# Two more products of h's part of n placed between the copy of the first gate product's bank and its second use

## The chip, the cores and the metric

The kernel runs on one core of one Trainium2 chip. The metric is the device time of one execution in microseconds (us). The time before is the median of three runs.

## What is computed

The reference has two layers over 128 graphs of 128 nodes with 256 features, all in float32. The change lies in the last step of layer 0, a gated unit. Cut to that part:

```python
h = relu(layernorm(x))
x_conv = ...                      # a convolution over the nodes of h
x_nmp  = ...                      # messages weighted by exp(-distance)
gi = concat([x_conv, x_nmp]) @ w_ih.T + b_ih
gh = h @ w_hh.T + b_hh
r = sigmoid(gi_r + gh_r)
z = sigmoid(gi_z + gh_z)
n = tanh(gi_n + r * gh_n)
x = x + (1 - z) * n + z * h
```

So r and z need one sum of three products each (of h, of the convolution and of the messages), while n needs h's product (gh_n) apart from the other two, because r multiplies it. "h's part of n" is that product, gh_n. Layer 1 is a graph convolution over 25 nodes of each graph.

## The kernel before, in words

The graphs are taken in 32 groups of four. `stage_c(q)` computes the gated unit of group q. The left operands are features on partitions, so h, the messages and the convolution of a group are tiles `hT`, `xm` and `xc` of 128 partitions by 2 by 512.

Each product of a 2 by 2 block weight matrix with a 2 by 2 block activation is done as seven products of sums of blocks in place of eight products of blocks. The sums of weights are made once (`fold_gates`: `wrz` for r and z, `wn` for n from messages and convolution, `wh` for n from h). The sums of activations are made per group on VectorE (`sums`: tiles `th`, `tm`, `tc`). In `stage_c`, `part(ps, w, i, xs, first, last)` issues the matmuls of product i into a PSUM bank `ps`, and `product` takes a bank and does a whole product in it. `factor` chooses the block or the sum for slot i. One matmul of 128 rows by 256 columns in float32 is two instructions in the profile. A part of `wrz` over one source is two matmuls (four instructions), and a product of `wh`, which has one source and half the width, is one matmul (two instructions).

PSUM has three banks in the pool `pgat` (the gates' banks `p1`, `p6`, `p5`, and later products in the same three) and five in the pool `ptmp` (tag "tmp"), which all other work shares.

The order around the change, by the lines of the kernel before:

- L741: product 0 of the r and z gates is ended in bank `p1`, by the convolution's part of it.
- L742: ScalarE copies `p1` to `u2`, because product 0 is wanted alone as well.
- L743 to L745: VectorE makes the four sums `tc` of the convolution.
- L757 to L759: product 0 of h's part of n is made in the bank `h1` (from `ptmp`), and ScalarE copies it to `va`.
- L761: product 1 of the gates is added into the same bank `p1` (its second use), over h, messages and convolution: six matmuls, twelve instructions.
- L762: ScalarE takes the sigmoid of `p1`, which gives the first half of r.
- L764 to L766: product 5 is ended in `p6`, VectorE adds it to `u2`; product 1 of h's part of n is added into `h1`, and `gate` multiplies it with r.
- L769 and L770: product 4 is ended in `p5`; product 5 of h's part of n is made and VectorE adds it to `va`.
- L777 to L780: product 6 of the gates is made, VectorE forms `u3` and `z2`; product 6 of h's part of n is made and VectorE writes `vb = va + product`.
- L785 to L796: products 3, 2 and 4 follow, product 2 in bank `p5` for the second time.

The copies `u2` share their SBUF place (tags `u2`, `u3`) with the tiles `d` of the step's end (L832 to L836), which GpSimd reads.

The order of the whole program is written out when it is built. Each piece of work is a generator in a `Lane`, and `Order.run` picks the lane that has had the least TensorE time for its weight, among those that are due. A `yield a, b` says that the piece has put a microseconds of work on TensorE and is due again b microseconds later. So the numbers in the yields decide where the other lanes' instructions are placed between the pieces of `stage_c`: the rest of the message work (`early`), the normalization before layer 1 (`rows`) and layer 1 itself (`prepare`, `block`). In the transposes that end group q-1 (`po`, L853) the same lane comes back to an earlier group.

Of the kernel before, what the change touches and what calls it, by code (L numbers as in the profile page):

```python
# [11 lines left out]
ALU = mybir.AluOpType  # L12
# [195 lines left out]
def kernel(ctx: ExitStack, tc: tile.TileContext, x, adj, consts, vecs, w_se, conv1_w,  # L208
                    conv2_w, w_msg, b_msg, w_ih, w_hh, W1, W2, b2, fusion_w, out):
    nc = tc.nc  # L210
# [7 lines left out]
    ptmp = ctx.enter_context(tc.tile_pool(name="ptmp", bufs=5, space=PSUM))  # L218
# [336 lines left out]
    def some_sums(q, n):  # L555

        if q in IN:
            if q not in SUMS:
                hT, xm = IN[q]
                (th, a), (tm, b) = sums("th", q, hT), sums("tm", q, xm)  # L560
                SUMS[q] = th, tm, a + b
            while SUMS[q][2] and n != 0:
                SUMS[q][2].pop(0)()
                n = n and n - 1
# [92 lines left out]
    def stage_c(q):  # L657
# [38 lines left out]
        wrz, wn, wh = LATE["wrz"], LATE["wn"], LATE["wh"]  # L696
# [6 lines left out]
        def part(ps, w, i, xs, first, last, again=False):  # L703


            n = [(m, o) for o in xs for m in range(w.shape[3] // P)]
            for j, (m, (k, x, t)) in enumerate(n):
                nc.tensor.matmul(ps[:, m], w[:, i, k, m * P:(m + 1) * P], factor(i, x, t),  # L708
                                 start=first and j == 0, stop=last and j == len(n) - 1,
                                 skip_group_check=again)  # L710

        def product(w, i, xs, pool=pgat):
            ps = bank(w, i, pool)
            part(ps, w, i, xs, True, True)
            return ps

        def bank(w, i, pool=pgat):
            return pool.tile([P, w.shape[3] // P, D], FP, tag="gat" if pool is pgat else "tmp",
                             name=f"p{w.shape[3]}{q}_{i}")

        def sigmoid(dst, src, b):
            for m in range(2):
                nc.scalar.activation(dst[:, m], src[:, m], AF.Sigmoid, bias=brz[:, b + m:b + m + 1])  # L723
# [23 lines left out]
        xs, xh = [(0, hT, th), (2, xm, tm), (1, xc, tcs)], [(0, hT, th)]  # L747

        ve = fr.tile([P, 3, 1, D], FP, tag="ve", name=f"ve{q}")
        va, vb, vt = ve[:, 0], ve[:, 1], ve[:, 2]  # L750
# [6 lines left out]
        h1 = bank(wh, 0, ptmp)  # L757
        part(h1, wh, 0, xh, True, True)
        nc.scalar.activation(va, h1, AF.Copy)  # L759
        yield 0.43, 0.0  # L760
        part(p1, wrz, 1, xs, False, True, True)  # L761
        sigmoid(r1, p1, 0)  # L762
        yield 2.6, 0.0
# [3 lines left out]
        gate(r11, h1, 0)  # L767
        yield 1.3, 0.0
        part(p5, wrz, 4, xs[2:], False, True)  # L769
        nc.vector.tensor_tensor(va, va, product(wh, 5, xh, ptmp), ALU.add)  # L770
        some_sums(q + 1, 2)
        yield 1.3, 0.0
        while q and q - 1 not in C_DONE:
            yield 0.0, 0.5
        z = fr.tile([P, 2, 512], FP, tag="z", name=f"z{q}")
# [1 line left out]
        nc.vector.tensor_tensor(u3, u2, product(wrz, 6, xs), ALU.add)  # L777
        nc.vector.tensor_tensor(z2, u3, p5, ALU.add)  # L778
        sigmoid(z2, z2, 2)
        nc.vector.tensor_tensor(vb, va, product(wh, 6, xh, ptmp), ALU.add)  # L780
        some_sums(q + 1, 2)
        yield 3.03, 0.0
        xt = fr.tile([P, 4, D], FP, tag="xt", name=f"xt{q}")
        load_x(xt, q)
        nc.vector.tensor_tensor(z1, u3, product(wrz, 3, xs), ALU.add)  # L785
# [322 lines left out]
    for bat, (during_a, during_b) in enumerate(((0.66, 0.5), (0.2, 0.65))):  # L1108
# [12 lines left out]
        tc.tile_pool(name="co", bufs=1, side="right", reuse_waits="tile"))  # L1121
    loads = Lane([stage_n(q) for q in range(NQ)])
    groups = Lane([stage_c(q) for q in range(NQ)], ahead=2)
    second = [setup_1()] + [part(blk) for blk in range(NBLK) for part in (prepare, block)]
    beside.weight = 0.5
# [43 lines left out]
```

## Time and profile before

| what | value |
|---|---|
| three runs | 2124.36, 2126.18 and 2129.8 us, median 2126.18 us |
| profiled execution, its own time | 2123.29 us |
| its span in the profile | 2121.2 us |
| mean granted TensorE clock | 0.989 |
| TensorE: matmuls busy, weight loads busy | 2056.6 us (97%), 1656.3 us (78%) |
| VectorE, ScalarE, GpSimd busy | 1177.2 us (55%), 687.6 us (32%), 723.2 us (34%) |
| first and last copy `u2` (L742) | at 730.9 us and at 2001.6 us, 32 copies |

The page gives one profiled execution. The groups' gated units take the stretch from about 724 us to the end, with layer 1 interleaved. In the profile's rows, PE is a matmul and PEld is the loading of its weights; an idle time is followed by an arrow to what ended it. Instructions are named by line and by output<-input tile; `p<-hTc,wrz` is a matmul with h as the moving operand, out of `wrz`, into a gate's bank.

### The profile page before, as it was taken

How to read it: one execution, taken by the hardware profiler on the slowest of the kernel's cores; microseconds unless marked ns; L12 is line 12 of the kernel's file. 1: busy time of each engine (PE TensorE's matmuls, PEld its weight loads, DVE VectorE, ACT ScalarE, POOL GpSimd, SP SyncE). 2: the span in 40 equal slices, each digit the busy share in tenths (PEclk: the TensorE clock that was granted, in tenths of full speed). 3: DMA queues.
4: the chain of work that ended last, by engine and by line, in shares of the span. 5: the costliest groups of instructions: out<-in, count | busy, mean ns of one | idle time of the engine just before them, and what ended most of it. 6: DMA issues, size and time to landing. Idle time of an engine off the chain costs nothing.

```text
span 2121.2 us, 30965 instructions
## 1 busy us (share of the span) xinstructions
PE 2056.6 (97%) x11316; PEld 1656.3 (78%) x11316; DVE 1177.2 (55%) x2775; ACT 687.6 (32%) x1543; POOL 723.2 (34%) x900
## 2 busy tenths in 40 slices
PE   6998999999999999999999999999999999999998
PEld 5566888789888787787778777878787787778775
DVE  5665444786544455645654654566455555654542
ACT  3554222344222233332232332232233323223233
POOL 2442666231565123422332233233213323233230
PEclk9999999999999999999999999999999999999999
DMA  9997778744787534233223232323222332323121
GB/s 182 264 269 231 242 267 261 213 145 150 254 267 253 184 110 153 61 100 77 73 71 83 84 83 71 107 73 78 80 82 75 83 97 75 78 80 102 36 68 50
DMA packets 187050, 281.66 MB, mean 133 GB/s; under 512 B 20685, under 2 KB 140242, under 8 KB 186898
## 3 DMA queue, kind: packets, MB, share of 16 engines
q1 hardware_dynamic: 156066, 184.81, 31.2%
q0 software_dynamic: 30000, 94.13, 13.7%
q8 instruction: 90, 1.47, 0.3%
q10 hardware_dynamic: 832, 0.74, 0.2%
q14 instruction: 62, 0.51, 0.1%
HBM read 187.34 MB, written 92.27 MB: 132 GB/s over the span
## 4 chain that ended last, share of the span: by engine, by line
PE 88%; DVE 3%; DMA 3%; POOL 2%; ACT 2%; issue 1%; SPq 0%; POOLq 0%; DVEq 0%; ACTq 0%
PE p L708 39%; PE pa L501 7%; PE pm L600 5%; PE ph L1029 5%; PE pz L1038 5%; PE pc L397 4%; PE pb L501 3%; PE pf L408 3%; PE px L626 3%; PE pi L673 2%; PE pg L1072 1%; DMA wfd<-ws 1%; PE po L853 1%; PE ph L386 1%; PE pw L450 1%
## 5 line engine op out<-in xcount | busy, mean ns | idle before, releaser
L833 POOL TENSOR_TENSOR d<-hTc,r 128x512 f32<-128x512 f32 x64 | 81.4, 1272 | 371.1 <-ACT r L830 371.1
L501 PE MATMUL pa<-wf,X 128*128 128x256 f32 x640 | 152.4, 381 | 0.0
L862 POOL DMA_DIRECT2D out<-xt x128 | 71.8, 566 | 204.2 <-DVE xt L859 201.5
L723 ACT ACTIVATE z<-z,brz 128x256 f32<-128x256 f32 x128 | 58.1, 501 | 253.3 <-DVE z L778 205.6
L524 DVE SCALAR_TENSOR_TENSOR y<-pa,kk 128x512 f32<-128x512 f32 x78 | 53.8, 690 | 147.4 <-ACT kk L523 147.4
L708 PE MATMUL p<-th,wrz 128*128 128x256 f32 x512 | 131.8, 380 | 0.0
L708 PE MATMUL p<-tc,wrz 128*128 128x256 f32 x512 | 131.6, 379 | 0.0
L708 PE MATMUL p<-tm,wrz 128*128 128x256 f32 x512 | 131.4, 379 | 0.0
L501 PEld LDWEIGHTS pa<-wf,X 128*128 128x128 f32 x640 | 118.1, 190 | 16.4 <-issue 2.2
L397 PE MATMUL pc<-c1w,hTa 128*128 128x256 f32 x512 | 124.4, 389 | 3.5 <-ACT ef L588 2.3
L600 PE MATMUL pm<-wmsg,hT 128*128 128x256 f32 x512 | 124.0, 388 | 0.0
L690 DVE SCALAR_TENSOR_TENSOR xc<-pc,s_bn,hTc 128x256 f32<-128x256 f32 x128 | 53.1, 477 | 117.3 <-PE pc L687 117.3
L708 PE MATMUL p<-hTc,wrz 128*128 128x256 f32 x384 | 106.1, 399 | 10.1 <-ACT u L742 10.1
L397 PEld LDWEIGHTS pc<-c1w,hTa 128*128 128x128 f32 x512 | 95.3, 194 | 22.2 <-DVE h L400 4.0
L1029 PE MATMUL ph<-yz,w 128*128 128x96 f32 (+3 forms) x640 | 111.5, 329 | 0.9 <-DVE yz L1014 0.9
L708 PEld LDWEIGHTS p<-hTc,wrz 128*128 128x128 f32 x384 | 68.3, 191 | 55.6 <-ACT u L742 22.5
L600 PEld LDWEIGHTS pm<-wmsg,hT 128*128 128x128 f32 x512 | 97.4, 193 | 16.7 <-issue 1.6
L1031 ACT ACTIVATE hh<-ph,vec 128x96 f32<-128x96 f32 (+3 forms) x160 | 64.3, 403 | 139.8 <-PE ph L1029 130.9
L1038 PE MATMUL pz<-hh,w 128*128 128x96 f32 (+3 forms) x640 | 107.7, 322 | 0.0
L708 PEld LDWEIGHTS p<-tm,wrz 128*128 128x128 f32 x512 | 97.3, 190 | 13.2
L1029 PEld LDWEIGHTS ph<-yz,w 128*128 128x128 f32 x640 | 90.1, 197 | 21.8 <-issue 15.5
L708 PEld LDWEIGHTS p<-th,wrz 128*128 128x128 f32 x512 | 94.5, 190 | 12.6 <-issue 0.6
(203 smaller groups left out, 4590.4 us busy)
## 6 DMA issues: line engine op xcount, KB each, us to landing
wf<-wfd SPq DMA_DIRECT2D x160, 256.0 KB, 3.9
wfd<-ws POOLq DMA_DIRECT2D x64, 320.0 KB, 7.3
yd<-y POOLq DMA_DIRECT2D x80, 256.0 KB, 3.7
yt<-yd SPq DMA_DIRECT2D x64, 320.0 KB, 4.9
w<-in_W SPq DMA_DIRECT2D x40, 512.0 KB, 3.6
xa<-in_x SPq DMA_DIRECT2D x128, 128.0 KB, 5.0
hTd<-hTa POOLq DMA_DIRECT2D x32, 512.0 KB, 5.0
hT<-hTd SPq DMA_DIRECT2D x32, 512.0 KB
```

Of the source, the lines that this page charges most:

```text
L397: nc.tensor.matmul(pc[:, i], hT[:, k, (2 * h + i) * N:(2 * h + i + 1) * N], c1w[:, k], start=(k == 0), stop=(k == 1))
L408: nc.tensor.matmul(pf[:, i, :F * NB], h1[:, 2 * h + i, k * P:(k + 1) * P], fwd, start=True, stop=True)
L501: nc.tensor.matmul(ps, xk(k), WF[f][:, k, s], start=(k == 0), stop=(k == 1))
L600: nc.tensor.matmul(pm[:, i], hT[:, k, j * N:(j + 1) * N], LATE["wmsg"][:, k], start=(k == 0), stop=(k == 1))
L626: nc.tensor.matmul(px[:, dc, i], msgs[h][:, i, dc * P:(dc + 1) * P], aT[:, 2 * h + i], start=True, stop=True)
L708: nc.tensor.matmul(ps[:, m], w[:, i, k, m * P:(m + 1) * P], factor(i, x, t), start=first and j == 0, stop=last and j == len(n) - 1, skip_g ...
L723: nc.scalar.activation(dst[:, m], src[:, m], AF.Sigmoid, bias=brz[:, b + m:b + m + 1])
L833: nc.gpsimd.tensor_sub(d, hT[:, dc], r[:, dc])
L862: nc.gpsimd.dma_start(out=out[q * GB + j, WIDE:].rearrange("(t n) c -> n t c", n=WIDE), in_=xt[j * WIDE:(j + 1) * WIDE, 1:4])
L1029: nc.tensor.matmul(ph, w1[:, k, m * P:(m + 1) * P], yz[:, k, :, o:o + n], start=(k == 0), stop=(k == 1))
L1031: nc.scalar.activation(hh[:, m], ph, AF.Relu, bias=v("b1", g * 4 + m))
L1038: nc.tensor.matmul(pz, w2[:, g, m, cc * P:(cc + 1) * P], hs[g][:, m], start=(m == 0), stop=(m == 3))
```

## The change

The products 5 and 6 of h's part of n are made earlier: directly after product 0 of h's part of n, ahead of the second use of `p1`. Both take banks of `ptmp`. The two additions on VectorE go with them. The yields of the three pieces are changed by the same amounts, so that their sum stays the same to 0.01. Nothing is added and nothing is left out.

```diff
         h1 = bank(wh, 0, ptmp)
         part(h1, wh, 0, xh, True, True)
         nc.scalar.activation(va, h1, AF.Copy)
-        yield 0.43, 0.0
+        h6, h7 = product(wh, 5, xh, ptmp), product(wh, 6, xh, ptmp)
+        nc.vector.tensor_tensor(va, va, h6, ALU.add)
+        nc.vector.tensor_tensor(vb, va, h7, ALU.add)
+        yield 1.3, 0.0
         part(p1, wrz, 1, xs, False, True, True)
         sigmoid(r1, p1, 0)
         yield 2.6, 0.0
@@ -767,9 +770,8 @@
         gate(r11, h1, 0)
         yield 1.3, 0.0
         part(p5, wrz, 4, xs[2:], False, True)
-        nc.vector.tensor_tensor(va, va, product(wh, 5, xh, ptmp), ALU.add)
         some_sums(q + 1, 2)
-        yield 1.3, 0.0
+        yield 0.87, 0.0
         while q and q - 1 not in C_DONE:
             yield 0.0, 0.5
         z = fr.tile([P, 2, 512], FP, tag="z", name=f"z{q}")
@@ -777,9 +779,8 @@
         nc.vector.tensor_tensor(u3, u2, product(wrz, 6, xs), ALU.add)
         nc.vector.tensor_tensor(z2, u3, p5, ALU.add)
         sigmoid(z2, z2, 2)
-        nc.vector.tensor_tensor(vb, va, product(wh, 6, xh, ptmp), ALU.add)
         some_sums(q + 1, 2)
-        yield 3.03, 0.0
+        yield 2.6, 0.0
```

## The prediction

> **What bounds the kernel now.** I read the page's busy times first, then its costliest groups, then the weight loads and the chain around one copy of `u2`, then the same place in all 32 groups.
>
> ```profile
> PE 2056.6 (97%) x11316; PEld 1656.3 (78%) x11316; DVE 1177.2 (55%) x2775; ACT 687.6 (32%) x1543; POOL 723.2 (34%) x900
> PE 88%; DVE 3%; DMA 3%; POOL 2%; ACT 2%; issue 1%; SPq 0%; POOLq 0%; DVEq 0%; ACTq 0%
> ...
> L708 PE MATMUL p<-hTc,wrz 128*128 128x256 f32 x384 | 106.1, 399 | 10.1 <-ACT u L742 10.1
> ...
> L708 PEld LDWEIGHTS p<-hTc,wrz 128*128 128x128 f32 x384 | 68.3, 191 | 55.6 <-ACT u L742 22.5
> ```
>
> TensorE is the bound: 97% busy, 88% of the chain that ended last. So only what makes TensorE stand still, or do more, counts. In the third and fourth row h's matmuls of the gates stand idle for the copy `u2` at L742: 10.1 us by the matmuls' rows, 22.5 us by the weight loads'. The list of waits, TensorE's weight loads alone, gives the number of cases:
>
> ```profile
> PEld p L708 <- ACT u L742: 22.5, 31, 0.8
> PEld p L708 <- PE pi L673: 19.5, 24, 0.8
> PEld p L708 <- DVE r L823: 7.2, 13, 2.2
> PEld p L708 <- DVE ve L796: 6.1, 28, 0.3
> ```
>
> It happens in 31 of 32 groups, 0.8 us at most. Group 24 shows one case, first its weight loads, then its piece of the chain:
>
> ```profile
> 1720.25 0.84 PEld L708 LDWEIGHTS p<-xc,wrz 128*128 128x128 f32 x4
> 1721.11 0.41 PEld L708 LDWEIGHTS p<-hTc,wh 128*128 128x128 f32 x2
> 1722.23 0.73 PEld L708 LDWEIGHTS p<-hTc,wrz 128*128 128x128 f32 x4 [0.72 <-ACT u L742]
> 1722.99 0.84 PEld L708 LDWEIGHTS p<-xm,wrz 128*128 128x128 f32 x4
> 1723.85 0.84 PEld L708 LDWEIGHTS p<-xc,wrz 128*128 128x128 f32 x4
> ```
>
> ```profile
> 1719.98 1.53 PE p L708 x7
> 1721.50 0.02 issue
> 1721.52 0.02 ACTq L742
> 1721.54 0.04 issue
> 1721.59 0.61 ACT u L742
> 1722.19 0.04 issue
> 1722.24 1.78 PE p L708 x7
> ```
>
> Product 0 ends at 1721.50, ScalarE copies the bank until 1722.19, and the same bank's next matmul starts at 1722.24. Between stands only h1's one matmul (two instructions). The chain runs through the copy, so the wait is on the path that sets the end.
>
> [...]0.04 us lie between the copy's end and the matmul. [...]In group 2 the trace shows it already: there matmuls of the messages happen to stand between, and no idle time is seen. [...]
>
> **Part 1: the wait at `p1` is covered.** Spacing of the stream: four weight loads take 1723.85 - 1722.99 = 0.86 us, so 0.2165 us for an instruction. From the start of h1's load (1721.11) to that of `p<-xm` (1722.99) are six instructions: 6 x 0.2165 = 1.30 us if nothing waits, 1.88 us in fact. The loss is 0.58 us, less than the 0.72 us of idle[...]. By the same two starts in each group: 0.52 us in group 0 (730.50 to 732.32), nothing in group 2, 0.65 us in the five groups 11, 16, 21, 26 and 31 (group 26: 1798.85 to 1800.80), and 0.58 us in the other 25. Sum 0.52 + 5 x 0.65 + 25 x 0.58 = 18.3 us. The ends for this unknown are the two sums of idle time: 10.1 us (matmul rows) and 22.5 us less a normal gap of 0.03 us each, 21.6 us. I take 18.3, since it is the delay of the instructions that follow.
>
> Is the cover long enough? Two products are four instructions, 0.87 us. The load of `p<-hTc` would come at 1721.11 + 6 x 0.2165 = 1722.41, when it was released at 1722.23: 0.18 us to spare. In the five groups where the copy starts 0.06 us later (it waits there for GpSimd's L836, whose input has the same place as `u2`) some 0.11 us are left. So all of it goes. If GpSimd fell behind TensorE by the time gained, these five would keep at most 0.5 us each, 2.5 us in all.
>
> **Part 2: what is taken from where the products stood.** TensorE's work is the same. Product 6 of the gates now follows product 4, and product 3 product 6, without the 0.43 us of a product of h's part between them. Their banks and what frees them, in group 24: product 6 takes `p1`'s bank, free when the sigmoid ends (1726.03, moved to about 1726.3), wanted at 1728.0; product 3 takes `p6`'s, free after VectorE's L765 (1727.63, then about 1727.9), wanted at 1730.6; product 2 goes into `p5` after L778 (1732.60, then about 1732.4), wanted at 1734.22 - 0.58 = 1733.6. Margins 1.7, 2.7 and 1.2 us: cost nothing. If the last cover is gone, it is 0.1 us for each 0.1 us beyond.
>
> **Part 3: the two additions on VectorE.** 421 and 414 ns (L770, L780), only moved. They now wait for the copy `va` (ends 1722.46) and for two matmuls, so they run from about 1722.5 to 1723.3. VectorE has nothing to do there from 1720.42 (end of the sums `tc`) to 1725.57. Queued behind them are the additions of `po` and L765, which wait for later matmuls anyhow. The adders also free two of the five shared banks; in the order of the built program the transposes `po` of the group before take these banks and wait for them. They stand at about 1725.0: 1.7 us to spare. Cost nothing. The new matmuls' own banks are free: from group 5 on the built order has them wait for nothing but TensorE's own earlier writes, in group 1 for VectorE's L618, which ended at 774.47 where they are due at 774.5. No DMA and no GpSimd or SP instruction changes its place in the built order.
>
> **Part 4: the other lanes.** In the built order groups 8 to 31 are the same but for the two products. In groups 2 to 7 the yields shift pieces of layer 1. Two places look worse. Group 3: five small reductions (L955, which wait for GpSimd) go ahead of the additions of `po` on VectorE.
>
> ```profile
> 859.07 0.41 DVE L856 TENSOR_TENSOR x<-xt,po 128x256 f32<-128x256 f32 x1
> 859.86 0.54 POOL L950 TENSOR_TENSOR b<-aj,cst 25x48 f32<-25x48 f32 x2
> 860.33 1.26 DVE L955 TENSOR_REDUCE dg<-b 25x16 f32<-25x400 f32 x5
> 861.52 0.67 DVE L765 TENSOR_TENSOR u<-u,p 128x512 f32<-128x512 f32 x1
> ```
>
> GpSimd ends at 860.40, so the reductions end at about 861.7, the three additions (1.3 us) at 863.0, L765 at 863.7. Product 3 wants that bank at 864.28 - 0.58 = 863.7: between 0 and 0.3 us. Group 4: three `py` and `po` come between the new products and `p1`; the third `py` takes the bank of product 5, freed after the sums `tc` (893.17 to 894.8) and an addition, at 895.2, where it is due at 894.8; `po` then waits for ScalarE's copy of the first. I price both at 0.5 us. Groups 5 to 7: pieces change places without a new wait that I see; plus or minus 2 us for all early groups, from the largest single idle time there (2.2 us, the wait for L823).
>
> **Sum.** 18.3 - 0.2 - 0.5 = 17.6 us. The profiled execution took 2123.29 us (span 2121.2 and 2.1 around it), so 2105.7. It was 2.9 us below the median of the runs, 2126.18; against that, 2108.6, or 0.83% less. The runs spread from 2124.36 to 2129.8. About 0.3% (6.4 us) is what a measurement of this kernel can tell from no change.
>
> **Rivals.**
>
> A, the gap moves on: TensorE runs ahead of the others by the time gained and loses part of it at the next waits (L796 in 28 groups, L823, the five groups with GpSimd). For it: these waits exist already, though short, 6.1 and 7.2 us in all. Against it: their releasers start from TensorE's own matmuls, so they move along. If half is lost: 2126.2 - 9 = 2117.
>
> B, nothing is gained: the ends of matmuls are modelled, and the idle time could be one of the record. Against it: starts are measured, and the loads after it are late by 0.58 us, while in group 2 they are not. 2126, plus or minus 3.
>
> C, slower: three temporary banks are held by one group at once, and `po` now waits for the second addition on VectorE. If VectorE came to it late, TensorE would stand at `po` in order. It costs from 1.7 us late on, and decides from 1.7 + 0.58 = 2.3 us. At 3 us late it is 1.3 - 0.58 = 0.7 us more in each of 31 groups: 2126.2 + 22 = 2148. Against it: VectorE is idle there for 5 us in group 24, and the built order has the additions at the head of its queue.
>
> That the change does not do what it says is excluded by the built order: the two products follow h1 in all 32 groups.
>
> **How the numbers follow.** Forecast 0.82, A 0.09, B 0.05, C 0.04. The forecast's own range: 18.3 with its ends 10.1 and 21.6 and the early groups' 2 us, narrowed to what the starts allow, 2103 to 2113; A carries it to 2116, and a low median takes one more below: 2102 to 2116. Faster by over 0.3% (below 2119.8): the forecast and nearly all of A, 0.90. Within 0.3%: B and a little of A, 0.06. Slower: 0.04.
>
> **What would show it.** Right: the row of `p<-hTc,wrz` no longer names ACT u L742, or with under 2 us; from the start of h1's load to that of `p<-xm` ten instructions, 2.17 us without a gap; PE's busy time the same within 0.5%, with the span 17 to 18 us shorter; from group 8 on 0.58 us less a group; VectorE's two additions about 0.9 us after product 0's end, and no idle at `po`. Wrong: a wait of 0.1 us or more left at `p1` (cover too short); new idle time before `po` or product 3 in the late groups; the early groups longer by more than 2 us.

## The result and the profile after

The changed kernel takes 2104.2 us (median of four runs, 2103.5 to 2107.3) against 2127.6 us for the kernel before beside it (2124.4 to 2129.8): ratio 0.9904, 95% interval 0.9886 to 0.9923 (the two medians divided give 0.989, inside the interval). A second measurement beside the later experiments gave 0.9916 (0.9901 to 0.9932). The profiled execution took 2104.03 us, its span is 2102.1 us; the forecast made against the profiled execution was 2105.7.

From the page of the changed kernel, the busy times, the chain that ended last and the row of h's gate matmuls:

```profile
PE 2046.5 (97%) x11316; PEld 1656.8 (79%) x11316; DVE 1180.4 (56%) x2775; ACT 687.3 (33%) x1543; POOL 723.3 (34%) x900
...
PE 91%; DMA 3%; DVE 3%; issue 1%; POOL 1%; ACT 0%; SPq 0%; POOLq 0%; DVEq 0%; ACTq 0%
...
L708 PE MATMUL p<-hTc,wrz 128*128 128x256 f32 x384 | 103.7, 393 | 0.0
```

The work is the same (11,316 matmul instructions). The copy has left the chain (ACT from 2% to 0%), and the row's idle time went from 10.1 us to nothing. The waits of the weight loads of the changed kernel, for the products of the gated unit (total us, number of cases, the longest):

```profile
PEld p L708 <- PE pi L673: 19.5, 24, 0.8
...
PEld p L708 <- DVE r L824: 7.2, 13, 2.2
PEld p L708 <- DVE ve L797: 6.5, 28, 0.4
```

The row for `ACT u` (22.5 us, 31 cases) is gone, and the other three stand as before: the wait was not handed on to them. Group 24 in the changed kernel, TensorE's weight loads, ScalarE and VectorE put together in order of time (start, duration, instruction, and in brackets the idle time before it with what ended it):

```profile
1708.44 0.41 PEld L708 LDWEIGHTS p<-hTc,wh 128*128 128x128 f32 x2
...
1708.88 0.84 PEld L708 LDWEIGHTS p<-th,wh 128*128 128x128 f32 x4
1708.92 0.60 ACT L742 ACTIVATE u<-p 128x512 f32<-128x512 f32 x1 [2.59 <-PE p L708]
...
1709.74 0.84 PEld L708 LDWEIGHTS p<-hTc,wrz 128*128 128x128 f32 x4
1709.82 0.42 DVE L761 TENSOR_TENSOR ve<-ve,p 128x256 f32<-128x256 f32 x1 [2.08 <-ACT ve L759]
...
1710.35 0.42 DVE L762 TENSOR_TENSOR ve<-ve,p 128x256 f32<-128x256 f32 x1
1710.60 0.84 PEld L708 LDWEIGHTS p<-xm,wrz 128*128 128x128 f32 x4
```

The new products (`p<-th,wh`, four instructions) lie beside the copy. From h1's load to that of `p<-xm` are 1710.60 - 1708.44 = 2.16 us for ten instructions: no gap. The two additions run 0.9 to 1.9 us after the copy's start, while VectorE has nothing else.

**Where the time came from.** The interval from one copy `u2` to the next measures one group. But a single profile has stretches of about 3.4 us in which the granted TensorE clock is 0.5, and not at the same places in every execution. Two windows of 4 us, of the changed kernel and then of a second profile of the same program:

```profile
904.00:908.00 4.00, 3.33 (x25) 2.77 (x23) 3.35 (x9) 1.83 (x5) 0.00 (x0) 0.99 0.00 0
908.00:912.00 4.00, 4.00 (x12) 3.50 (x13) 1.18 (x6) 0.35 (x1) 2.06 (x3) 0.58 0.01 4
```

```profile
904.00:908.00 4.00, 3.45 (x24) 2.86 (x23) 3.35 (x9) 1.91 (x5) 0.00 (x0) 1.00 0.03 5
908.00:912.00 4.00, 3.88 (x19) 3.52 (x20) 1.58 (x7) 0.42 (x2) 2.06 (x3) 1.00 0.02 4
```

The third number from the end is the clock: 0.58 against 1.00, 12 matmul instructions against 19. The time lost is (1 - 0.58) x 4 = 1.7 us, and group 4 is 1.67 us longer in the first profile. In the groups without such a stretch the two profiles agree to 0.02 us. So I sum (1 - clock) x 4 over the windows of 4 us from the first copy to 2088 us and take it off the time from the first copy to the end. "Without clock" below is this time:

| kernel | first copy to end | lost to the clock | without clock |
|---|---|---|---|
| before | 1390.3 | 8.5 | 1381.8 |
| changed, first profile | 1373.4 | 8.5 | 1364.9 |
| changed, second profile | 1370.2 | 5.1 | 1365.1 |

The change is worth 16.8 us in the trace (0.8%); the prediction had 17.6. The remaining 2.3 us between the first two spans (19.1) lie ahead of the first copy, where the two profiles of the changed kernel also differ, by 1.8 us. The runs' own difference is 16 to 24 us by the interval.

By group, changed kernel (second profile) less before, half-clock stretches taken out: -0.53, -0.58, -0.01, -0.58 in groups 0 to 3; +1.37 and +0.27 in groups 4 and 5; -1.45, -0.97, -0.77 in 6 to 8; then -0.58 in most groups (-0.65 in 11, 16, 21 and 26; about -0.5 in 13, 18, 23 and 28).

### The profile page after: what moved, and what is told of

The parts are those of the page before. It is cut to its first block, busy times and chain, and to the rows that moved or that the text cites. A ratio compares the mean times of both kernels' runs of the same rounds, so it can differ in the third digit from the quotient of the medians.

```text
span 2102.1 us, 31046 instructions
## 1 busy us (share of the span) xinstructions
PE 2046.5 (97%) x11316; PEld 1656.8 (79%) x11316; DVE 1180.4 (56%) x2775; ACT 687.3 (33%) x1543; POOL 723.3 (34%) x900
## 4 chain that ended last, share of the span: by engine, by line
PE 91%; DMA 3%; DVE 3%; issue 1%; POOL 1%; ACT 0%; SPq 0%; POOLq 0%; DVEq 0%; ACTq 0%
PE p L708 42%; PE pa L501 7%; PE pm L600 5%; PE ph L1030 5%; PE pz L1039 5%; PE pc L397 4%; PE pb L501 3%; PE pi L673 3%; PE px L626 3%; PE pf L408 2%; DMA wfd<-ws 2%; PE pg L1073 1%; PE pc L687 1%; PE po L854 1%; PE ph L386 1%; PE py L1013 1%
## 5 line engine op out<-in xcount | busy, mean ns | idle before, releaser
L723 ACT ACTIVATE z<-z,brz 128x256 f32<-128x256 f32 x128 | 58.1, 501 | 225.1 <-DVE z L780 190.9
L708 PEld LDWEIGHTS p<-tc,wrz 128*128 128x128 f32 x512 | 95.0, 190 | 12.1 <-issue 0.5
```

## The experiments

Each kernel was run several times beside the kernel before. Theory: the gain is the wait at `p1`, covered by just enough TensorE work. Rivals: the gap is only one of the record, so that nothing is lost in it (B); the gain comes from moving the products away from their old places, or from the yields.

**One product instead of two.**

```diff
         nc.scalar.activation(va, h1, AF.Copy)
-        yield 0.43, 0.0
+        h6 = product(wh, 5, xh, ptmp)
+        nc.vector.tensor_tensor(va, va, h6, ALU.add)
+        yield 0.87, 0.0
```

(product 6 stays at its old place)

> Only product 5 of h's part of n is moved up; product 6 stays where it was before. Theory (the two products cover the wait for the copy of p1): one product is 0.43 us of cover for a delay of 0.58 us, so 0.43 of it goes in 31 groups, 13.3 us: about 2114 us, a wait for ACT u of some 0.25 us left in each group. Rival 1 (anything put between removes the wait whole): as the changed kernel, 2104 to 2108. Rival 2 (what gains is the rearranged order of the other lanes): nothing to do with the amount of cover, 2104 to 2127 with no wait row to match.

Measured: 2109.8 us, ratio 0.9931 (0.9917 to 0.9946); without clock 1369.7, 12.1 less than before (expected 13.3; the early groups gave less). The weight loads of this kernel in one late group:

```profile
1714.80 0.41 PEld L708 LDWEIGHTS p<-hTc,wh 128*128 128x128 f32 x2
1715.23 0.41 PEld L708 LDWEIGHTS p<-th,wh 128*128 128x128 f32 x2
1715.92 0.73 PEld L708 LDWEIGHTS p<-hTc,wrz 128*128 128x128 f32 x4 [0.28 <-ACT u L742]
1716.68 0.84 PEld L708 LDWEIGHTS p<-xm,wrz 128*128 128x128 f32 x4
```

A wait of 0.28 us is left. Each late group is 0.43 us shorter than before, half-clock stretches apart: the two instructions (2 x 0.2165) that now fill the gap. Of the 0.58 us, 0.15 are still lost. Cover pays one for one until the gap is full.

**Both products moved, but behind the second use of `p1`.**

```diff
-        yield 0.43, 0.0
         part(p1, wrz, 1, xs, False, True, True)
         sigmoid(r1, p1, 0)
-        yield 2.6, 0.0
+        h6, h7 = product(wh, 5, xh, ptmp), product(wh, 6, xh, ptmp)
+        nc.vector.tensor_tensor(va, va, h6, ALU.add)
+        nc.vector.tensor_tensor(vb, va, h7, ALU.add)
+        yield 3.9, 0.0
```

(their old places are emptied as in the change; 3.9 is the sum of the three pieces)

> Both products are moved up as in the change, but put directly behind the second use of p1 in place of ahead of it. Theory: nothing covers the copy, so the wait is there again in 31 groups (22 us by weight loads) and the time is that of the kernel before, within 3 us. Rival (the gain is that VectorE's two additions leave the later, busier place, or that other lanes lie better): most of the gain stays, 2105 to 2112.

Measured: 2126.7 us, ratio 1.001 (0.9997 to 1.0023). From its list of waits:

```profile
PEld p L708 <- ACT u L742: 24.7, 31, 2.9
```

The wait is back and the gain is gone. Group by group the difference to before is 0.00 to 0.04 us, half-clock stretches apart, except once (group 8, told below). So leaving the old places is worth nothing; the gain needs the place ahead of `p1`.

**A third product as well.** Product 3 of h's part of n, which stood behind product 3 of the gates, follows the other two (its old place is emptied, and that yield falls from 3.03 to 2.6):

```diff
         nc.vector.tensor_tensor(vb, va, h7, ALU.add)
-        yield 1.3, 0.0
+        nc.vector.tensor_tensor(vt, vb, product(wh, 3, xh, ptmp), ALU.add)
+        yield 1.73, 0.0
```

> Product 3 of h's part of n, with its addition, is moved up too, so that 1.30 us lie between copy and second use in place of 0.87. Theory: the wait is already covered by two (0.18 us to spare), so nothing more is gained: the changed kernel's time within 2 us, or a little more where the fourth shared bank has to be waited for. Rival (more cover gains more): 5 to 13 us less than the changed kernel.

Measured: 2107.3 us, ratio 0.9929 (0.9917 to 0.994). No wait for `ACT u`; 0.58 us less than before in the settled groups (the late ones, where the other lanes keep their order), as with two. More cover than the gap earns nothing. Without clock it is 1367.7, some 2.7 us more than the changed kernel; between groups 7 and 14 the pieces of layer 1 have moved, by up to 8 us to one group and back from the next. Half of the 2.7 us lies in group 3: a load of `p<-th,wrz` waits 1.58 us there for ScalarE's sigmoid (L723), a wait that no other kernel has. The sigmoid starts late, behind a table load of 1.28 us on ScalarE and, before that, a piece of layer 1. The other half, in groups 7 to 14, stays open.

**Two more products, not used, in the kernel before.** This kernel does extra work: products 5 and 6 are made twice, and nobody reads the first ones.

```diff
         nc.scalar.activation(va, h1, AF.Copy)
-        yield 0.43, 0.0
+        product(wh, 5, xh, ptmp), product(wh, 6, xh, ptmp)
+        yield 1.3, 0.0
```

> The kernel before, with two more products in the place that are never read (products 5 and 6 of h's part of n are made twice): TensorE has 128 more instructions of 0.2165 us, 27.7 us of work. Theory (TensorE really stands still for 0.58 us there): the 18.3 us of standing are filled, so the kernel is slower by 27.7 - 18.3 = 9.4 us, 2137. Rival B (the idle time is one of the record only): slower by the whole 27.7 us, 2155.

Measured: 2137.0 us, ratio 1.0067 (1.0055 to 1.0079), which is 14.2 us above before by the ratio and 12.9 by the medians. The expected 2137 was hit by luck: it was 9.4 us above a starting point of 2127.6, and the kernel before took 2124.1 here. Groups 24 to 27 are 0.28, 0.28, 0.23 and 0.28 us longer, where the work alone is 4 x 0.2165 = 0.87: so 0.59 us of it is free. At 0.28 that makes some 9 us over 32 groups; the rest is in the early groups, where the order of the lanes moves and new waits appear (2.8 us once for `ACT u`, whose copy waits for GpSimd, 1.6 us once for `ACT xc`). Rival B falls: had the gap cost nothing, each of these groups would be 0.87 us longer.

**How much spare is there?** The changed kernel, with the copy released later by a second copy of a part of the same bank ahead of it: half of it, or one column. The changed kernel itself ran beside them. The edit for the half copy (that for one column is alike):

```diff
+        nc.scalar.activation(u2[:, 0:1], p1[:, 0:1], AF.Copy)
         nc.scalar.activation(u2, p1, AF.Copy)
```

> The changed kernel itself, once more, as the yardstick for the three kernels beside it on the same chip. Expected as in its first measurement: 0.9904 of the kernel before, 2103 to 2107 us, no wait of h's gate matmuls for the copy of product 0.

> The changed kernel, but ScalarE copies the first half of the bank p1 to u2 once more, ahead of the whole copy. The values are the same; only the bank comes free later. The same half copy of another bank takes 378 ns in the profile, so with the step between two instructions some 0.40 us. My theory: the two products leave 0.18 us to spare (0.11 in five groups), so 0.22 to 0.29 us of idle come back in 31 groups: 2.5 to 7 us above the changed kernel of this call (the lower end if a short idle costs less than itself, as 0.72 us of idle cost 0.58), and the wait for ACT u is back in the list, 5 to 9 us in 31 cases. Rival, the spare is ample[...]: as the changed kernel within 1 us, no such wait.

> The same with a copy of one column ahead of the whole copy: about 0.16 us by the line through the copies of 256 and 512 columns (378 and 597 ns), with the step some 0.18 to 0.2 us. My theory: the spare is just used up, 0 to 0.1 us of idle in a group, so 0 to 2.5 us above the changed kernel of this call; the wait for ACT u, if it appears, under 3 us. Rival as for the half copy: nothing at all. A third case, the spare was less than I worked out: 4 us or more.

Measured: changed kernel again 2106.9 us (0.9916); half 2108.8 us, ratio 0.9938 (0.9925 to 0.9951); one column 2103.4 us, 0.9905 (0.9891 to 0.9918). Without clock 1365.1, 1369.5 and 1364.8. The half copy delays the copy by 0.42 us and costs 0.13 or 0.14 us in the usual group, 0.20 to 0.22 in the five with GpSimd: 4.4 us. The column delays it by 0.20 us and costs 0.00 to 0.01. The loads of the half copy's kernel, then of the column's:

```profile
1712.26 0.84 PEld L708 LDWEIGHTS p<-th,wh 128*128 128x128 f32 x4
1713.37 0.73 PEld L708 LDWEIGHTS p<-hTc,wrz 128*128 128x128 f32 x4 [0.27 <-ACT u L743]
1714.12 0.84 PEld L708 LDWEIGHTS p<-xm,wrz 128*128 128x128 f32 x4
```

```profile
1707.76 0.84 PEld L708 LDWEIGHTS p<-th,wh 128*128 128x128 f32 x4
1708.65 0.81 PEld L708 LDWEIGHTS p<-hTc,wrz 128*128 128x128 f32 x4
1709.48 0.84 PEld L708 LDWEIGHTS p<-xm,wrz 128*128 128x128 f32 x4
```

Four instructions take 0.866 us, so `p<-hTc` is due at 1713.13 and comes 0.24 us late; `p<-xm`, due at 1713.99, comes 0.13 late. In the second it is 0.03 late and the next load is on time. The spare is thus 0.42 - 0.24 = 0.18 us, or 0.20 - 0.03 = 0.17: the prediction had 0.18. And up to 0.11 us of a late load is recovered, here as in the kernel before (0.69 late, 0.58 lost) and with one product (0.26 late, 0.15 lost).

**Can the rule find more?** The next wait of this form is `h5`'s second use, which waits 0.21 to 0.36 us, in most cases 0.22, for VectorE's addition (L797) in 28 groups. The changed kernel, with product 5 of n put between, and the yields made to fit:

```diff
-        part(h5, wh, 2, xh, False, True, True)
-        nc.vector.tensor_tensor(va, va, h5, ALU.add)
-        yield 1.3, 0.2
-        nc.vector.tensor_tensor(v2, v1, product(wn, 5, xs), ALU.add)
+        n5 = product(wn, 5, xs)
+        part(h5, wh, 2, xh, False, True, True)
+        nc.vector.tensor_tensor(va, va, h5, ALU.add)
+        yield 2.17, 0.2
+        nc.vector.tensor_tensor(v2, v1, n5, ALU.add)
...
-        yield 0.87, 0.2
+        yield 0.0, 0.2
```

> The changed kernel, with the second use of the bank h5 (product 2 of h's part of n) placed behind product 5 of n instead of ahead of it, so that two more matmuls cover the addition that empties h5 (VectorE's ve at L797: 28 cases, 6.5 us of idle by the weight loads, 0.22 to 0.3 us each). My theory, that idle time in TensorE's order is worth about what the following instructions are late by: the wait of 28 groups goes, 2 to 6 us below the changed kernel of this call, about 2101. Rival: so short an idle [...]delays nothing, within 1 us of the changed kernel, though the row of waits goes. Second rival: the pieces of the message work that the yield lets in come at another place, and a new wait takes it back, 0 to 4 us above.

Measured: 2106.9 us, 0.9927 (0.9913 to 0.994), beside 2106.9 of the changed kernel. The row of waits is gone; without clock 1362.2, 2.9 us less. The runs do not show so little, and the expected median of about 2101 was missed. That the 2.9 us lie in the expected 2 to 6 is no proof: groups are up to 15 us shorter and the next ones longer, since the yields moved other lanes' pieces, so what the wait itself was worth can't be read here. Two kernels separate the yields from the order. The first is the changed kernel with the old yields:

```diff
-        yield 1.3, 0.0
+        yield 0.43, 0.0
...
-        yield 0.87, 0.0
+        yield 1.3, 0.0
...
-        yield 2.6, 0.0
+        yield 3.03, 0.0
```

> The changed kernel with the three yields of the kernel before (0.43, 1.3 and 3.03 us). The built order then differs from the changed kernel's in groups 0 to 5 alone: in group 4 the pieces of layer 1 no longer come between the new products and the second use of p1. What is tested is the loss in the early groups: in the changed kernel groups 4 and 5 are 1.4 and 0.3 us longer than before, where 0.58 us less was due. My theory, the third and fourth py that wait 0.48 and 0.82 us make most of it: those two waits go or shrink, and groups 3 to 8 together are 1 to 2 us shorter than in the changed kernel, half-clock stretches taken out; groups 9 to 31 the same to 0.02 us each. In the runs this is too small to be seen: 0.990 to 0.993 of the kernel before. Rival, the loss is the shorter stretch of TensorE work for layer 1's VectorE and ScalarE pieces, whatever their order: groups 3 to 8 the same in sum within 0.5 us.

Measured: 2102.3 us, 0.990 (0.9883 to 0.9916). From the weight loads of layer 1 in group 4, the changed kernel first, then this one:

```profile
892.92 0.66 PEld L1013 LDWEIGHTS py<-r,x1h 128*128 128x128 f32 x4 [0.48 <-DVE ve L761]
...
907.98 1.21 PEld L1013 LDWEIGHTS py<-r,x1h 128*128 128x128 f32 x4 [0.82 <-ACT x1h L935]
```

```profile
897.34 2.20 PEld L1013 LDWEIGHTS py<-r,x1h 128*128 128x128 f32 x12
```

The three `py` now follow `p1`'s products without a wait, and the last one waits 0.22 us in place of 0.82. Against the changed kernel, half-clock stretches out: group 4 -1.97 us, group 5 -0.85, groups 6 to 8 +0.86, +0.54 and +0.29; sum -1.2. Groups 9 to 30 are the same to 0.02 us where no half clock falls. With the old yields groups 3 to 8, too, are 0.4 to 0.6 us shorter than before, each by itself. So the gain does not come from the changed yields; they cost some of it.

The second moves `h5`'s second use behind product 5 of n with the yields left at 1.3 and 0.87:

```diff
-        part(h5, wh, 2, xh, False, True, True)
-        nc.vector.tensor_tensor(va, va, h5, ALU.add)
         yield 1.3, 0.2
-        nc.vector.tensor_tensor(v2, v1, product(wn, 5, xs), ALU.add)
+        n5 = product(wn, 5, xs)
+        part(h5, wh, 2, xh, False, True, True)
+        nc.vector.tensor_tensor(va, va, h5, ALU.add)
+        nc.vector.tensor_tensor(v2, v1, n5, ALU.add)
```

> As the last kernel, with h5's second use behind product 5 of n, but with the yields left as they are, so that the pieces of the other lanes stay nearly where they were. Before it the trace was 3.4 us shorter in groups 8 to 30 and 2.6 us longer after the last copy, where pieces had moved; so that the gain in TensorE's own order stood against moved pieces. My theory, about 0.14 us of any such idle time costs nothing and the rest is lost (0.72 us of idle cost 0.58, 0.29 us cost 0.14): 28 waits of 0.22 to 0.30 us are worth 0.08 to 0.15 us each, so 2 to 4 us less from the first copy on than in the changed kernel, and the row of waits for ve gone. Rival, they cost nothing: within 0.5 us from the first copy on. In the runs 0.988 to 0.992 of the kernel before, which can't tell the two apart; the trace has to.

Measured: 2106.5 us, 0.9915 (0.9897 to 0.9932). The row for `ve` is gone, and each settled group is 0.07 to 0.09 us shorter (0.13 to 0.17 in a few), as 0.22 us of recorded idle less 0.14 asks. (Its list has 4.8 us for `x1h` in 14 cases: 0.39 us ahead of a load of `tm` for n, which the changed kernel has too and puts down to `v` or to nothing.) Yet without clock it is 1365.0, no less than the changed kernel. A new wait in group 8 holds the gain; ScalarE's copy there, then GpSimd's last operation ahead of it:

```profile
1072.03 0.60 ACT L742 ACTIVATE u<-p 128x512 f32<-128x512 f32 x1 [4.82 <-POOL z L838]
```

```profile
1070.67 1.33 POOL L838 TENSOR_TENSOR z<-d,r 128x512 f32<-128x512 f32 x1
```

`u2` shares its place with GpSimd's `d`, so the copy waits until GpSimd is done at 1072.00; h's gate matmuls then idle 2.1 us. In most other groups the idle time ahead of the copy is 2.59 us and ends with product 0. Both favoured edits together (old yields, `h5` behind product 5) came next:

> The changed kernel with the yields of the kernel before and with h5's second use behind product 5 of n: the two edits that the traces so far favour, together. From the yields about 1.2 us less in groups 3 to 8 than in the changed kernel (the two waits of py in group 4 are gone), from h5 about 0.08 us less in each of groups 8 to 31 (2 to 2.5 us), half-clock stretches taken out: from the first copy to the end 3 to 3.7 us less than in the changed kernel, about 0.985 to 0.990 of the kernel before in the runs, 2100 to 2104 us. Rival, as in the last kernel a new wait in one group (there 2.1 us for ACT u) gives the gain back: 0 to 1.5 us less from the first copy on.

Measured: 2103.2 us, 0.9913 (0.9898 to 0.9927); without clock 1363.9, 1.2 us less than the changed kernel: the rival, with the same 2.1 us in group 8. This wait in group 8 is found in exactly three of the 13 profiles so far: here, in the last kernel, and in the one with the products behind `p1`. They are the three without a half clock between 1040 and 1066 us. (The kernel with the unused products has a wait of the same form, 2.8 us, a group earlier.) In the others TensorE loses 3.4 us there (1.7 in three), and GpSimd is done in time, or nearly. The last kernel has both edits and gives the `d` that shared `u2`'s place one of its own:

```diff
-            d = fr.tile([P, 512], FP, tag=f"u{2 + dc}", name=f"d{q}_{dc}")
+            d = fr.tile([P, 512], FP, tag=("d0", "u3")[dc], name=f"d{q}_{dc}")
```

> The last kernel (both edits) with a place in SBUF of its own for the tile d that GpSimd reads at the step's end, which so far shares u2's place. TensorE's order is the same. What is tested: in the 13 traces so far, the copy u2 in the ninth group (about 1066 us) is held by GpSimd's z for 2.2 us in exactly the three runs in which the TensorE clock was not halved at 1040 to 1066 us; where it was, TensorE came 3.4 us later and GpSimd was done. My theory, the wait is real and is only hidden by the half clock: with its own place the copy no longer waits for GpSimd in any group, no wait of h's gate matmuls for ACT u is left whatever the clock does, and the five groups in which GpSimd ends the copy's wait lose the 0.06 us. From the first copy to the end, half-clock time taken out, 1.5 to 2.5 us less than in the last kernel if that clock is not halved there, and 0 to 0.5 us less if it is (then the clock takes 3.4 us). In the runs 0.988 to 0.992 of the kernel before. Rival: GpSimd is late as an engine, and the next thing that needs it waits as long: the same within 0.5 us.

Measured: 2104.1 us, 0.9909 (0.9888 to 0.9929); without clock 1362.0, and no half clock at 1040 to 1066. The copy in group 8, and GpSimd's operation that had held it:

```profile
1064.69 0.60 ACT L742 ACTIVATE u<-p 128x512 f32<-128x512 f32 x1 [2.52 <-PE p L708]
```

```profile
1065.62 1.33 POOL L838 TENSOR_TENSOR z<-d,r 128x512 f32<-128x512 f32 x1
```

The copy starts 0.93 us ahead of an operation that it used to wait for, and no later wait takes its place: 1.9 us less than the kernel with both edits, as expected. In no group does the copy wait for GpSimd any more. Of the kernels whose parts are all understood this is the shortest by the trace, 3 us (0.14%) below the changed kernel; the runs cannot tell it from the changed kernel.

## Why the prediction was right, and where its sizes were off

**Part 1 was right, in mechanism and size.** It took the delay of the following instructions (0.58 us), not the idle time in either row (0.32 or 0.72 us), and 0.58 is what most groups gained, 0.65 in the groups with GpSimd, nothing in group 2. The experiments carry it: one product fills as much of the gap as it lasts (0.43 us), a third gains nothing, the same products behind `p1` gain nothing (what stood behind the waiting matmuls did not run ahead of them: 24.7 us of waits in 31 cases), and products that nobody needs are free for 0.59 us. The spare of 0.18 us was 0.17 to 0.18. Why the second use of `p1` waits at all was not tested: the values ask for it, since product 1 is added to what stands in `p1` and `u2` must hold product 0 alone; whether anything else does, no run shows.

**Parts 2 and 3 were right.** The waits that existed kept their sizes, no new one for product 6, 3 or 2 of the gates is in the late groups, and VectorE did the additions in its idle time.

**Part 4 was too low.** It priced group 3 at 0 to 0.3 us and group 4 at 0.5 us. Group 3 lost nothing. In group 4 the third `py` waits 0.48 us, as worked out; but a later `py` also waits, 0.82 us where it was 0.21, for ScalarE's `x1h`, which the prediction did not follow. In sum groups 0 to 7 gained 2.5 us where 4.0 - 0.7 = 3.3 were forecast. The kernel with the old yields gives 1.2 us back. So the 17.6 us become 16.8. Part 4's range of 2 us covers the miss, but its reading of group 4 was incomplete.

**The time.** The forecast of 2108.6 us started from a median of 2126.2; 2104.2 lies 4.4 us below it, and the second median, 2106.9, 1.7. Beside the trace's 16.8 us, the first pair of medians differs by 23.4 us, the second by 17.6; medians of the same kernel moved by 3 to 5 us between measurements (before: 2122.9 to 2127.6), so the rest is not a mechanism that I can name.

**The rivals.** A (half lost at the next waits): not seen; L797 and L824 kept 6.5 and 7.2 us. B: refuted by the extra products. C: the `po` behind the additions shows no new wait. That GpSimd could hold the copy was in Part 1, for five groups at 0.06 us; that it holds one group by 2.2 us when the clock is not halved there could not be seen in the profile of before, whose clock was.

## What to carry to other kernels

When TensorE waits for a short copy of a bank that it uses again, put independent matmuls ahead of the wait, as long as the gap (here 0.87 us of work for a gap of 0.58 us; 1.30 us gained nothing more, and 0.87 us behind the wait gained nothing). Price the gap by how late the instructions behind it are (0.58 us), not by the idle time of either row (0.32 or 0.72 us). When a hand-written order follows stated costs, changing those costs is an edit of its own: try the move without it. When a gain of a few us is looked for in single profiles, compare group by group and take out the stretches of low clock.

## What the runs showed of the hardware

- The granted TensorE clock falls to 0.5 for 3.41 us at a time, now and then for twice that (6.83 us from 1056.8 us on in the kernel before, from 1054.7 us on in the changed kernel). From the first copy to 2088 us this takes 8.5, 8.5 and 5.1 us in the three profiles of the table. In the profiles of the kernel before, of the changed kernel (the first) and of the last experiment there are 12 falls in this stretch, four in each. Layer 1 starts a set of sixteen small matmuls `pa<-cst,b` (L961 in the kernel before; weights of 25x128, moving operand of 25x64, 2.0 us together) 2.3 to 3.4 us ahead of every one of them. In the first two profiles TensorE is booked as busy for all of the 3.41 us ahead of seven falls, and for 2.8 us ahead of the eighth. There are 8 such sets in an execution, 24 in the three, and no fall follows the other 12. The falls of one profile begin whole multiples of 3.413 us apart (131, 249 and 291 from the first one in the kernel before; 12, 55 and 300 in the changed kernel). On that grid the eight sets ahead of a fall in these two profiles start 0.05 to 1.12 us after a point, the other eight 1.43 to 2.42 us after one. So where a set begins on the grid goes with whether the clock falls, and it is not the same sets in each profile. No run changed these matmuls, so their part is read from the record and not tested. A fall can even hide a wait, as that of 2.1 us in group 8.
- Of the time by which the first load behind a wait comes late, up to 0.11 us is recovered at the next group of loads: 0.69, 0.26, 0.24 and 0.03 us late became 0.58, 0.15, 0.13 and 0.00 lost. In recorded idle time (0.72, 0.28, 0.27) the difference is 0.13 to 0.14 us. What recovers it, no run shows.
- ScalarE's copy out of PSUM with 128 partitions takes 171 ns for one column, 378 ns for 256 (377 to 384) and 597 ns for 512: between the last two 0.86 ns a column. The line through them would give one column 160 ns, 11 less than measured.
